# Order of the small tiled matmuls in a state-space block with adaptive layer norm: reversed groups, inter-chunk products behind C-B products, a ring of ten C buffers

## The chip, the cores and the metric

The kernel runs on one core of a Trainium2 chip. The metric is the device time of one launch in microseconds (us). Three runs of the kernel before took 587.96, 587.55 and 584.75 us; the median is 587.55 us.

## The reference

Four sequences (b) of 512 tokens with 256 channels go through one block. `mod` is computed from a condition vector; `xBC` goes through a causal convolution of four taps over the tokens; the scan has 32 heads of 8 channels with a state of 64; the feed-forward part has 1024 hidden channels and a Walsh-Hadamard transform.

```python
h = layernorm(x) * (1 + ca) + sa
xBC, z, A_log = split(h @ W_in.T)
x_, B, C = split(conv4(xBC) + conv_b)
a = -softplus(A_log)
L = exp(segsum(a))                              # lower triangle, 512 x 512 per head
M = einsum('blhn,bshn,bhls->bhls', C, B, L)
y = einsum('bhls,bshp->blhp', M, x_) + D * x_
x = x + ga * (y * silu(z + z_bias)) @ W_out.T
h = layernorm(x) * (1 + cb) + sb
x = x + gb * fwht(silu(h @ W1.T) * (h @ W3.T)) @ W2.T
```

All of it is in float32, and so is the output, (4, 512, 256).

## The kernel before

**Tiling.** The 512 x 512 matrices are never formed. Tokens are cut into 8 chunks of 64. Inside a chunk y comes from products of C and B with the decay (intra); between chunks a state of 64 x 8 per head is carried (states, a scan, inter). A projection (`proj`, L249) is six matmuls of 128 x 512 into one PSUM buffer: float32 is split in a high and a low part, and three of the four products are made for two halves of the 256 channels.

**Units, quads, pairs.** There are 8 units (i, b): half i of the heads, sequence b. A unit has two quads m; a quad has four pairs of heads. The pairs are numbered k from 0 to 63 over all units, four to a quad. So one step k is one pair, and one unit is eight steps.

**What a step does.** Names as they stand in the profile:

- `project(k, half)` (L432) makes B (tile pbc, L251) or C (tile pcc, L251) in PSUM. `conv` (L385) then convolves it into SBUF (bc or cc): ACT writes the first tap (L387) and a shifted copy cv (L389), DVE adds two taps (L390, L391) and with the second one has read the PSUM buffer for the last time, POOL adds cv (L392). Three PSUM buffers are shared by these projections and by px and pz. bc has a ring of 3 buffers and cc one of 8.
- `prep_l(k)` (L425): one matmul pl (L428) and ACT's Exp give the decay l (L430).
- `attend(k)`, at every odd k (L442): 64 small matmuls of 64 x 64 for the two pairs k-1 and k, in tiles pG (L262), each on a quarter of PE's array. They are chained in one order by `Chain` (L253). DVE then multiplies l by pG (L458).
- `turn_b(k)` (L460): four transposes bT (L464), copied by ACT to bt (L466).

**What a quad does,** after its four steps: `states(m)` (L525, tile ps, L530), 16 small matmuls on 32 columns each, needs bt of the four pairs and xwz; `intra(m)` (L537, tile py, L546), 32 small matmuls on 32 columns, needs l of the four pairs and xpad; `turn_states(m)` (L552) transposes the states (sT), DVE scans them over the chunks (sn, L559) and POOL masks them into sts (L563); `inter(m)` (L566, tile pi, L572), 28 small matmuls on 32 columns, needs sts and C of the quad's four pairs, whose buffers come free behind it.

**What a unit does.** `x_part2` and `x_part3` (L502 on) lay x out for the small products: transposes xt (L513), then DVE writes xpad (L517) and xwz (L520), for the two halves of the tokens one after the other. `gate_z` (L577) projects z (pz), and `gate_y` (L589) joins py, pi and the gate: DVE multiplies ex by pi (L593), where ex is the decay from the start of a chunk. For every sequence in the first four units a prologue does the layer norm (xn, L281), the transposes (pt, L291), and a softplus chain on ACT and DVE (pa, parts, L354). In the second four units `finish_unit` projects the output (po, L610) and prepares the second layer norm. Then come 32 steps of the feed-forward part (tile f, L251; tiles pdy and pdyi, L724), from about 456 us on.

**What sets the order.** Every step is put on an agenda with a due time in units of k (`T`, L399; the calls from L780), and the agenda is run in order of time. That gives the order in which instructions are issued. On PE, DVE, ACT and POOL a scheduler in the build then decides the final order from its own estimates of when operands are ready. It can't move an instruction ahead of one that it is told to stay behind: `behind(x)` (L85) puts what is issued inside it behind the recorded instruction `last[x]`. SP, which issues most DMAs, keeps the order of the agenda.

The lines around the change, as they stand before:

```python
        for n, pg in zip(ks, pgs):
            ve.tensor_tensor(lts[n], pg, lts[n], ALU.mult)
...
        for c in range(1, NC):
            for g in range(4):
                l = slice(Q * c, Q * c + Q)
                pe.matmul(pi[32 * g : 32 * g + 32, l], sts[pp][:, c - 1, g], ccs[4 * m + g][:, l],
```

Of the kernel before, what the change touches and what calls it, by code (L numbers as in the profile page):

```python
# [14 lines left out]
F32R = mybir.dt.float32r  # L15
BF16 = mybir.dt.bfloat16
AF = mybir.ActivationFunctionType
ALU = mybir.AluOpType
# [3 lines left out]
NB, S, DM = 4, 512, 256  # L22
NH, HD = 32, 8
Q = 64
NC = S // Q
# [5 lines left out]
def mamba_ffn(tc, ctx, u, c_t, wmod, win_t, cw, cb, zb, dsk, wo_t, w13_t, w2_t,  # L31
              k_ident, k_reset, k_dl, k_dr, k_had, k_own, out):
    nc = tc.nc
    ve, ac, gp, pe = nc.vector, nc.scalar, nc.gpsimd, nc.tensor
# [25 lines left out]
    def work(shape, name, tag, bufs=2, dtype=F32):  # L60
        return wk.tile(shape, dtype, name=name, tag=tag, bufs=bufs)

    def mtile(shape, name):
        return ps_m.tile(shape, F32, name=name, tag="m")

    def ptile(name):
        return ps_p.tile([128, S], F32, name=name, tag="p")
# [15 lines left out]
    last = {}  # L83

    def behind(*engines):  # L85
        stack = ExitStack()
        for e in engines:
            stack.enter_context(tc.issue_after(last[e].ins))
        return stack
# [67 lines left out]
    sts = [const.tile([128, NC - 1, 4, 32], F32, name=f"sts{pp}") for pp in range(2)]  # L157
# [36 lines left out]
    def fetch_quad(n, half, **kw):  # L194
        return fetch(win_t[:, 544 + 1024 * n : 544 + 1024 * n + 1024], 512 * half, 512, f"wq{n}", **kw)
# [53 lines left out]
    def proj(ps, w, c0, ht):  # L249
        for n, (a, b, k) in enumerate(TERMS):  # L250
            last[pe] = pe.matmul(ps, w[:, a, k, c0 : c0 + 128], ht[k][:, b], start=(n == 0), stop=(n == 5))  # L251
# [133 lines left out]
    def conv(ps, tl, dst):  # L385
        w = cw_sb[:, tl]
        ac.activation(dst, ps, AF.Identity, bias=cb_sb[:, tl : tl + 1], scale=w[:, 3:4])  # L387
        v = work([128, S], "cv", "cv", 3)
        last[ac] = ac.activation(v, ps, AF.Copy, scale=w[:, 0:1])  # L389
        ve.scalar_tensor_tensor(dst[:, 1:], ps[:, : S - 1], w[:, 2:3], dst[:, 1:], ALU.mult, ALU.add)  # L390
        last["conv"] = ve.scalar_tensor_tensor(dst[:, 2:], ps[:, : S - 2], w[:, 1:2], dst[:, 2:], ALU.mult, ALU.add)  # L391
        last[gp] = gp.tensor_tensor(dst[:, 3:], dst[:, 3:], v[:, : S - 3], ALU.add)  # L392
# [5 lines left out]

    T = dict(  # L399
        attend=0.12, turn_b=0.13, prep_l=-1.31, proj_b=-1.11, proj_c=-1, load_d=-3.13,  # L400
        states=-0.03, intra=0.1, turn=1.47, inter=2.53,
        x_proj=1.32, x0=-1.5, x1=2.12, x2=3.46, x3=3.77, gate_z=5.89, fin0=3.54, fin1=3.96, fin2=4.99, fin3=6.63,
        pro0=-11.83, pro1=-7.06, pro2=-4.93, pro3=-4.48, pro4=-3.88, next_ht=-3.77, pro04=0.27,
        quads=1.55, xz1=32.3, wo=19.68, mod=18.99, w2=40.89, wf0=56.74, wf1=62.02, wf2=62.29,
# [3 lines left out]
    def where(k):  # L408
        i, b = units[k // 8]
        return i, b, (k // 4) % 2, k % 4  # L410

    lts, bcs, ccs, bts, exs, des, xcs, xds, dcs, stt, pys, zts = ({} for _ in range(12))
# [19 lines left out]
    def project(k, half):  # L432
        i, b, pp, g = where(k)
        w = wq[2 * i + pp]
        tl = 2 + 8 * (2 * i + pp) + 2 * g
        dct, nm, nb = ((bcs, "bc", 3), (ccs, "cc", 8))[half]
        pb = ptile(f"p{nm}{k}")
        proj(pb, w, 256 * g + 128 * half, ht[i, b])
        dct[k] = work([128, S], f"{nm}{k}", nm, nb)
        conv(pb, tl + half, dct[k])  # L440

    def attend(k):  # L442


        ks = (k - 1, k)
        pgs = [mtile([128, S], f"pG{n}") for n in ks]
        chain = Chain()
        for c in range(NC):


            for n, pg in list(zip(ks, pgs))[::-1]:
                for j in range(2):
                    i, o = 64 * j, 64 * (j ^ (n % 2))
                    r, l = slice(i, i + 64), slice(Q * c, Q * c + Q)
                    chain.matmul(pg[o : o + 64, l], bcs[n][r, l], ccs[n][r, l], start=True, stop=True,
                                 tile_position=(i, o))
        for n, pg in zip(ks, pgs):
            ve.tensor_tensor(lts[n], pg, lts[n], ALU.mult)  # L458

    def turn_b(k):  # L460
        bc = bcs[k]
# [63 lines left out]
    def states(m):  # L525
        pp = m % 2
        pst = mtile([128, 4, 128], f"ps{m}")
        for t in range(4):
            for g in range(4):
                pe.matmul(pst[32 * g : 32 * g + 32, t], xwz[:, t, 4 * g + 2 * pp : 4 * g + 2 * pp + 2].rearrange("p h q x -> p (h q x)"),  # L530
                          bts[4 * m + g][:, t], start=True, stop=True, tile_position=(0, 32 * g))
        for g in range(4):
            bts.pop(4 * m + g)
        stt[m] = work([128, 4, 128], f"st{m}", "st", 1)
        ac.activation(stt[m], pst, AF.Copy)

    def intra(m):  # L537
        n, pp = divmod(m, 2)
        if pp == 0:
            pys[n] = (ps_1.tile([128, S], F32, name=f"py{n}", tag="y"),  # L540
                      ps_1.tile([128, S], F32, name=f"pi{n}", tag="yi"))
        py = pys[n][0]
        for c in range(NC):
            for g in range(4):
                l = slice(Q * c, Q * c + Q)
                pe.matmul(py[32 * g : 32 * g + 32, l], xpad[:, pp, c, g], lts[4 * m + g][:, l],  # L546
                          start=(pp == 0 and c == 0), stop=(pp == 1), skip_group_check=True,
                          tile_position=(0, 32 * g))
        for g in range(4):
            lts.pop(4 * m + g)  # L550
# [15 lines left out]
    def inter(m):  # L566
        n, pp = divmod(m, 2)
        pi = pys[n][1]
        for c in range(1, NC):
            for g in range(4):  # L570
                l = slice(Q * c, Q * c + Q)
                pe.matmul(pi[32 * g : 32 * g + 32, l], sts[pp][:, c - 1, g], ccs[4 * m + g][:, l],  # L572
                          start=(pp == 0 and c == 1), stop=(pp == 1), skip_group_check=True,
                          tile_position=(0, 32 * g))
        for g in range(4):
            ccs.pop(4 * m + g)

# [68 lines left out]
            split(wf[h], c0, 512, fetch(w13_t[:, 1024 * h : 1024 * h + 1024], c0, 512, f"wf{h}"))  # L646


    early = dict(tag="cc", bufs=8)
    q00 = fetch_quad(0, 0, **early)  # L650
    nc.sync.dma_start(wa, win_t[:, 512:544].rearrange("(k p) c -> p k c", p=128))
    cw_sb = cload(cw, [128, 34, 4], "cw_sb", nc.sync)
# [30 lines left out]
    for k in range(AHEAD):  # L683
        for half in range(2):
            with behind(pe, ve):
                project(k, half)
        if k == 1:
            with behind(ac):
                split_quad(1, 0, q10)
# [15 lines left out]
    def ffn_up(b, f):  # L705
        w = wf[f // 4]
        p1, p3 = ptile(f"f1{b}{f}"), ptile(f"f3{b}{f}")
        proj(p1, w, 256 * (f % 4), h2[b])
        proj(p3, w, 256 * (f % 4) + 128, h2[b])
        t = work([128, S], f"ft{b}{f}", "bt", 6)  # L710
        ac.activation(t, p1, AF.Tanh, scale=0.5)  # L711
        ve.scalar_tensor_tensor(t, t, 1.0, p1, ALU.add, ALU.mult)  # L712
        ve.tensor_tensor(t, t, p3, ALU.mult)  # L713
        hi = work([128, S], f"fh{b}{f}", "cc", 8, F32R)
        lo = work([128, S], f"fl{b}{f}", "cc", 8, F32R)
        ac.activation(hi, t, AF.Copy)  # L716
        (ve if (b, f) == (NB - 1, 7) else gp).tensor_tensor(lo, t, hi.bitcast(F32), ALU.subtract)  # L717
        return hi, lo
# [21 lines left out]
    def up(s_):  # L740
        hid[s_] = ffn_up(s_ // 8, s_ % 8)
# [38 lines left out]
    for m in range(16):  # L780
        at_time(4 * m + 4 + T["states"], states, m)
        at_time(4 * m + 4 + T["intra"], intra, m)
        at_time(4 * m + 4 + T["turn"], turn_states, m)
        at_time(4 * m + 4 + T["inter"], inter, m)
        if m:
            at_time(4 * m + T["load_d"], load_d, m)
    for k in range(NP):
        if k % 2:
            at_time(k + T["attend"], attend, k)
        at_time(k + T["turn_b"], turn_b, k)  # L790
        if k >= AHEAD:
            at_time(k + T["proj_b"], project, k, 0)
            at_time(k + T["proj_c"], project, k, 1)
        if k >= LOOK_P:
            at_time(k + T["prep_l"], prep_l, k)
# [112 lines left out]
```

## Time and profile before

| what | value |
|---|---|
| runs | 587.96, 587.55, 584.75 us |
| median | 587.55 us |
| profiled execution | 587.68 us |
| its span, first to last instruction | 585.9 us |
| mean granted clock of PE | 0.988 |
| PE, matmuls | 549.5 us busy |
| PE, weight loads (beside matmuls) | 432.6 us busy |
| DVE | 401.7 us busy |
| ACT | 387.2 us busy |
| POOL | 325.8 us busy |

Engines: PE multiplies matrices, DVE and ACT work elementwise (ACT with functions), POOL is a third elementwise engine, SP issues DMAs. L251 is line 251 of the kernel. A group line of a view has the line, the engine, and output and inputs by the program's names. In a row of the timeline the first number is the start in us from the start of the span and the second the length; "x6" are six instructions in a row, and a bracket at the end gives the idle time ahead of it and what ended it. In a row of the waits there are the engine and tile that waited, an arrow to what they waited for, the sum in us, how many times, and the longest one. In a row of the windows there are the stretch, its length, the busy time of PE, PE's weight loads, DVE, ACT and POOL (with instructions in brackets), the granted clock of PE, and the share and rate of the DMAs.

Some durations that come up: a tap on DVE takes 0.74 us (L390, L391), a product of l 0.68 us (L458), the scan of the states 1.21 us (L559), the four operations of xn on ACT 2.08 us (L281), the convolution's first tap on ACT 0.78 us (L387).

### The profile page before, as it was taken

What the parts mean: (1) busy time and instruction counts of PE and PEld (TensorE: products, weight loads), DVE (VectorE), ACT (ScalarE), POOL (GpSimd) and SP (SyncE); (2) the same over time, 40 slices, a digit from 0 to 9 for tenths busy, and PEclk for the clock granted to TensorE, in tenths of its full rate; (3) what the DMA queues carried; (4) which work ended last, traced back from release to release, by engine and by line L of the source; (5) the groups of instructions that cost most, each with busy time, mean ns of one, the idle gap of its engine ahead of it and who ended that gap; (6) DMA issues with size and microseconds to landing.
All of it is one profiled execution on the core that took longest, in us unless ns stands there. A gap on an engine that the chain in (4) does not pass through costs nothing.

```text
span 585.9 us, 16301 instructions
## 1 busy us (share of the span) xinstructions
PE 549.5 (94%) x6867; PEld 432.6 (74%) x6868; DVE 401.7 (69%) x672; ACT 387.2 (66%) x666; POOL 325.8 (56%) x299
## 2 busy tenths in 40 slices
PE   9868899899899989999999899899989999999996
PEld 5545686667687766877777677677767898888886
DVE  5978667977878675889787779787855454333243
ACT  5988779788966877896794787769584242232321
POOL 5862447435635668466465557477666645334341
PEclk9998999999999989999999899999989999999999
DMA  7351101401232343014103142164157037004021
GB/s 230 106 184 35 49 2 74 66 16 59 67 63 56 117 143 121 2 62 137 42 4 113 75 112 104 61 170 149 38 156 286 2 127 217 35 1 152 1 82 36
DMA packets 41793, 51.99 MB, mean 89 GB/s; under 512 B 17943, under 2 KB 29941, under 8 KB 41721
## 3 DMA queue, kind: packets, MB, share of 16 engines
q1 hardware_dynamic: 41448, 50.96, 28.5%
q8 instruction: 54, 0.88, 0.6%
q14 instruction: 19, 0.15, 0.1%
q10 hardware_dynamic: 272, 0.00, 0.0%
HBM read 33.51 MB, written 17.44 MB: 87 GB/s over the span
## 4 chain that ended last, share of the span: by engine, by line
PE 40%; DVE 5%; ACT 4%; POOL 2%; issue 1%; DMA 1%; POOLq 0%; DVEq 0%
PE f L251 15%; PE pcc L251 4%; PE pdy L724 4%; PE pdyi L724 4%; PE pbc L251 3%; PE po L610 2%; PE pG L262 1%; PE py L546 1%; PE bT L464 1%; ACT xn L281 1%; PE ps L530 1%; PE pi L572 1%; DVE cc L390 1%; DVE bc L390 1%; PE pt L291 1%
## 5 line engine op out<-in xcount | busy, mean ns | idle before, releaser
L392 POOL TENSOR_TENSOR bc<-bc,cv 128x509 f32<-128x509 f32 x64 | 69.6, 1088 | 55.8 <-DVE bc L391 37.9
L251 PE MATMUL f<-h,wf 128*128 128x512 f32 x384 | 97.7, 395 | 0.0
L392 POOL TENSOR_TENSOR cc<-cc,cv 128x509 f32<-128x509 f32 x64 | 69.7, 1090 | 50.1 <-DVE cc L391 39.1
L251 PEld LDWEIGHTS f<-h,wf 128*128 128x128 f32 x384 | 69.2, 190 | 12.5
L717 POOL TENSOR_TENSOR fl<-ft,fh 128x512 fp32r<-128x512 f32 x31 | 40.0, 1293 | 57.8 <-ACT fh L716 55.1
L390 DVE SCALAR_TENSOR_TENSOR cc<-pcc,cw_sb,cc 128x511 f32<-128x511 f32 x64 | 47.6, 743 | 32.2 <-ACT cv L389 32.1
L387 ACT ACTIVATE cc<-pcc,cb_sb,cw_sb 128x512 f32<-128x512 f32 x64 | 50.2, 784 | 22.8 <-PE pcc L251 17.3
L251 PE MATMUL pcc<-ht,wq 128*128 128x512 f32 x192 | 55.8, 424 | 6.1 <-DVE bc L391 6.1
L387 ACT ACTIVATE bc<-pbc,cb_sb,cw_sb 128x512 f32<-128x512 f32 x64 | 50.1, 782 | 15.4 <-PE pG L262 14.0
L716 ACT ACTIVATE fh<-ft 128x512 fp32r<-128x512 f32 x32 | 20.2, 631 | 57.6 <-DVE ft L713 27.7
L712 DVE SCALAR_TENSOR_TENSOR ft<-ft,f 128x512 f32<-128x512 f32 x32 | 21.9, 688 | 52.4 <-ACT ft L711 52.3
L251 PE MATMUL pcc<-hr,wq 128*128 128x512 f32 x192 | 54.5, 417 | 2.9 <-DVE bc L391 2.2
L390 DVE SCALAR_TENSOR_TENSOR bc<-pbc,cw_sb,bc 128x511 f32<-128x511 f32 x64 | 47.6, 744 | 11.1 <-ACT cv L389 10.8
L251 PE MATMUL pbc<-hr,wq 128*128 128x512 f32 x192 | 52.4, 406 | 1.4 <-DVE cc L391 1.0
L251 PE MATMUL pbc<-ht,wq 128*128 128x512 f32 x192 | 51.7, 402 | 1.6 <-DVE bc L391 1.6
L251 PEld LDWEIGHTS pcc<-ht,wq 128*128 128x128 f32 x192 | 35.7, 196 | 19.1 <-DVE bc L391 7.0
L391 DVE SCALAR_TENSOR_TENSOR bc<-pbc,cw_sb,bc 128x510 f32<-128x510 f32 x64 | 47.5, 743 | 1.2
L391 DVE SCALAR_TENSOR_TENSOR cc<-pcc,cw_sb,cc 128x510 f32<-128x510 f32 x64 | 47.6, 743 | 1.0
L458 DVE TENSOR_TENSOR l<-pG,l 128x512 f32<-128x512 f32 x64 | 41.2, 683 | 8.3 <-PE pG L262 7.9
L464 PE MATMUL bT<-ident,bc 128*128 128x128 f32 x256 | 41.2, 283 | 4.6 <-ACT bt L466 2.4
L466 ACT ACTIVATE bt<-bT 128x512 f32<-128x512 f32 x64 | 38.8, 606 | 9.8 <-PE bT L464 9.5
L262 PEld LDWEIGHTS pG<-cc,bc 64*64 64x64 f32 x2048 | 34.8, 134 | 13.7 <-issue 9.7
(154 smaller groups left out, 1244.8 us busy)
## 6 DMA issues: line engine op xcount, KB each, us to landing
wq<-win_t SPq DMA_DIRECT2D x16, 256.0 KB
htd<-ht SPq DMA_DIRECT2D x8, 512.0 KB
hr<-htd SPq DMA_DIRECT2D x8, 512.0 KB
h2d<-ht SPq DMA_DIRECT2D x8, 512.0 KB
h<-h2d SPq DMA_DIRECT2D x8, 512.0 KB
x<-u SPq DMA_DIRECT2D x7, 512.0 KB
ex<-pd SPq DMA_DIRECT2D x8, 256.0 KB
ygd<-yg SPq DMA_DIRECT2D x4, 512.0 KB
```

The lines of the kernel that those rows point to most:

```text
L251: last[pe] = pe.matmul(ps, w[:, a, k, c0 : c0 + 128], ht[k][:, b], start=(n == 0), stop=(n == 5))
L262: self.before = pe.matmul(*args, **kw)
L387: ac.activation(dst, ps, AF.Identity, bias=cb_sb[:, tl : tl + 1], scale=w[:, 3:4])
L390: ve.scalar_tensor_tensor(dst[:, 1:], ps[:, : S - 1], w[:, 2:3], dst[:, 1:], ALU.mult, ALU.add)
L391: last["conv"] = ve.scalar_tensor_tensor(dst[:, 2:], ps[:, : S - 2], w[:, 1:2], dst[:, 2:], ALU.mult, ALU.add)
L392: last[gp] = gp.tensor_tensor(dst[:, 3:], dst[:, 3:], v[:, : S - 3], ALU.add)
L458: ve.tensor_tensor(lts[n], pg, lts[n], ALU.mult)
L464: pe.transpose(pt[:, t], bc[:, 128 * t : 128 * t + 128], ident)
L466: ac.activation(bts[k], pt, AF.Copy)
L712: ve.scalar_tensor_tensor(t, t, 1.0, p1, ALU.add, ALU.mult)
L717: (ve if (b, f) == (NB - 1, 7) else gp).tensor_tensor(lo, t, hi.bitcast(F32), ALU.subtract)
L724: last[pe] = pe.matmul(pds[t // 2][:, t % 2], hid[a][:, tok], w2h[f][:, w_], start=(f == 0 and t % 2 == 0 and m == 0), stop=(f == 7 and m ...
```

## The change

- The due time of `inter` goes from 2.53 to 3.13 steps after the quad, and its matmuls are put behind the last matmul of the latest `attend`, which `attend` now records.
- The ring of C goes from 8 buffers to 10. Early weight loads and the feed-forward part's hidden tiles, which use the same ring, are named with 10 too.
- `attend` multiplies l of the second pair first, and l of the first pair is put behind that.
- `states` goes through t and g backwards; `intra` goes through the chunks backwards and through the pairs in the order 2, 3, 0, 1, so that the matmul that starts the accumulation (`start`) is that of the last chunk.

In the changed file the lines behind L457 stand 2 to 5 lines further down.

```diff
--- before.py
+++ after.py
@@ -398,7 +398,7 @@
 
     T = dict(
         attend=0.12, turn_b=0.13, prep_l=-1.31, proj_b=-1.11, proj_c=-1, load_d=-3.13,
-        states=-0.03, intra=0.1, turn=1.47, inter=2.53,
+        states=-0.03, intra=0.1, turn=1.47, inter=3.13,
         x_proj=1.32, x0=-1.5, x1=2.12, x2=3.46, x3=3.77, gate_z=5.89, fin0=3.54, fin1=3.96, fin2=4.99, fin3=6.63,
         pro0=-11.83, pro1=-7.06, pro2=-4.93, pro3=-4.48, pro4=-3.88, next_ht=-3.77, pro04=0.27,
         quads=1.55, xz1=32.3, wo=19.68, mod=18.99, w2=40.89, wf0=56.74, wf1=62.02, wf2=62.29,
@@ -433,7 +433,7 @@
         i, b, pp, g = where(k)
         w = wq[2 * i + pp]
         tl = 2 + 8 * (2 * i + pp) + 2 * g
-        dct, nm, nb = ((bcs, "bc", 3), (ccs, "cc", 8))[half]
+        dct, nm, nb = ((bcs, "bc", 3), (ccs, "cc", 10))[half]
         pb = ptile(f"p{nm}{k}")
         proj(pb, w, 256 * g + 128 * half, ht[i, b])
         dct[k] = work([128, S], f"{nm}{k}", nm, nb)
@@ -454,8 +454,10 @@
                     r, l = slice(i, i + 64), slice(Q * c, Q * c + Q)
                     chain.matmul(pg[o : o + 64, l], bcs[n][r, l], ccs[n][r, l], start=True, stop=True,
                                  tile_position=(i, o))
-        for n, pg in zip(ks, pgs):
-            ve.tensor_tensor(lts[n], pg, lts[n], ALU.mult)
+        last["pG"] = chain.before
+        last["l"] = ve.tensor_tensor(lts[k], pgs[1], lts[k], ALU.mult)
+        with behind("l"):
+            ve.tensor_tensor(lts[k - 1], pgs[0], lts[k - 1], ALU.mult)
 
     def turn_b(k):
         bc = bcs[k]
@@ -525,8 +527,9 @@
     def states(m):
         pp = m % 2
         pst = mtile([128, 4, 128], f"ps{m}")
-        for t in range(4):
-            for g in range(4):
+
+        for t in range(4)[::-1]:
+            for g in range(4)[::-1]:
                 pe.matmul(pst[32 * g : 32 * g + 32, t], xwz[:, t, 4 * g + 2 * pp : 4 * g + 2 * pp + 2].rearrange("p h q x -> p (h q x)"),
                           bts[4 * m + g][:, t], start=True, stop=True, tile_position=(0, 32 * g))
         for g in range(4):
@@ -540,11 +543,11 @@
             pys[n] = (ps_1.tile([128, S], F32, name=f"py{n}", tag="y"),
                       ps_1.tile([128, S], F32, name=f"pi{n}", tag="yi"))
         py = pys[n][0]
-        for c in range(NC):
-            for g in range(4):
+        for c in range(NC)[::-1]:
+            for g in (2, 3, 0, 1):
                 l = slice(Q * c, Q * c + Q)
                 pe.matmul(py[32 * g : 32 * g + 32, l], xpad[:, pp, c, g], lts[4 * m + g][:, l],
-                          start=(pp == 0 and c == 0), stop=(pp == 1), skip_group_check=True,
+                          start=(pp == 0 and c == NC - 1), stop=(pp == 1), skip_group_check=True,
                           tile_position=(0, 32 * g))
         for g in range(4):
             lts.pop(4 * m + g)
@@ -566,12 +569,14 @@
     def inter(m):
         n, pp = divmod(m, 2)
         pi = pys[n][1]
-        for c in range(1, NC):
-            for g in range(4):
-                l = slice(Q * c, Q * c + Q)
-                pe.matmul(pi[32 * g : 32 * g + 32, l], sts[pp][:, c - 1, g], ccs[4 * m + g][:, l],
-                          start=(pp == 0 and c == 1), stop=(pp == 1), skip_group_check=True,
-                          tile_position=(0, 32 * g))
+
+        with behind("pG"):
+            for c in range(1, NC):
+                for g in range(4):
+                    l = slice(Q * c, Q * c + Q)
+                    pe.matmul(pi[32 * g : 32 * g + 32, l], sts[pp][:, c - 1, g], ccs[4 * m + g][:, l],
+                              start=(pp == 0 and c == 1), stop=(pp == 1), skip_group_check=True,
+                              tile_position=(0, 32 * g))
         for g in range(4):
             ccs.pop(4 * m + g)
 
@@ -646,7 +651,7 @@
             split(wf[h], c0, 512, fetch(w13_t[:, 1024 * h : 1024 * h + 1024], c0, 512, f"wf{h}"))
 
 
-    early = dict(tag="cc", bufs=8)
+    early = dict(tag="cc", bufs=10)
     q00 = fetch_quad(0, 0, **early)
     nc.sync.dma_start(wa, win_t[:, 512:544].rearrange("(k p) c -> p k c", p=128))
     cw_sb = cload(cw, [128, 34, 4], "cw_sb", nc.sync)
@@ -711,8 +716,8 @@
         ac.activation(t, p1, AF.Tanh, scale=0.5)
         ve.scalar_tensor_tensor(t, t, 1.0, p1, ALU.add, ALU.mult)
         ve.tensor_tensor(t, t, p3, ALU.mult)
-        hi = work([128, S], f"fh{b}{f}", "cc", 8, F32R)
-        lo = work([128, S], f"fl{b}{f}", "cc", 8, F32R)
+        hi = work([128, S], f"fh{b}{f}", "cc", 10, F32R)
+        lo = work([128, S], f"fl{b}{f}", "cc", 10, F32R)
         ac.activation(hi, t, AF.Copy)
         (ve if (b, f) == (NB - 1, 7) else gp).tensor_tensor(lo, t, hi.bitcast(F32), ALU.subtract)
         return hi, lo
```

## Prediction

> **What bounds it now.** The head of the page and its first part come first: the busy time of each engine over the span.
>
> ```profile
> span 585.9 us, 16301 instructions
> PE 549.5 (94%) x6867; PEld 432.6 (74%) x6868; DVE 401.7 (69%) x672; ACT 387.2 (66%) x666; POOL 325.8 (56%) x299
> ```
>
> PE works 94% of the span, so the kernel is bound by PE's own time, and a change can gain in two ways: by making the busy stretch shorter, or by taking from the 36 us in which PE stands idle. The profiled execution took 587.68 us, 1.8 us of it outside the span; that is 0.1 us above the median of the three runs (587.55), so I count from 587.68 and correct nothing.
>
> The granted clock by stretches comes next, because idle PE can be paid for twice.
>
> ```profile
> 49.40:52.80 3.40, 1.53 (x9) 0.90 (x9) 3.17 (x7) 3.17 (x6) 0.00 (x0) 1.00 0.19 43
> 52.90:56.30 3.40, 3.40 (x10) 2.58 (x10) 3.40 (x8) 3.39 (x7) 1.94 (x2) 0.50 0.21 27
> 72.00:456.00 384.00, 365.31 (x5575) 281.21 (x5574) 296.77 (x480) 292.14 (x503) 232.09 (x213) 0.99 0.29 88
> ```
>
> The column of 0.50 and 1.00 is PE's clock. After a stretch with 1.53 us of work in 3.40 came one at half clock. The same 0.50 stands for 3.4 us at 209.9, 325.95 and 435.2 us, each time behind a PE wait of 1.4 to 1.7 us. Such a window costs up to 1.7 us (half of 3.4). From 72 to 456 us PE is busy 365.3 of 384 us and no other engine is over 297.
>
> The Trainium skill ("TensorE: Matmul & The Clock Gate", Part 1) gives a free-running window of 3413 ns and an idle window as the condition for half clock; the rows agree on the length, but here a window that was 45% busy was enough.
>
> **What a change of matmul shape costs.** PE's timeline gives the price. Columns: start, length, then the line and tile. I read start to start, since ends are modelled.
>
> ```profile
> 14.23 1.52 PE L251 MATMUL pbc<-ht,wq 128*128 128x512 f32 x6
> 15.59 1.52 PE L251 MATMUL pcc<-ht,wq 128*128 128x512 f32 x6
> 16.95 1.52 PE L251 MATMUL px<-ht,wxz 128*128 128x512 f32 x6
> ```
>
> Six full matmuls with full ones before and behind: 1.36 us.
>
> ```profile
> 176.79 0.39 PE L428 MATMUL pl<-dr,dl 94*128 94x512 bf16 x1
> 177.12 0.99 PE L572 MATMUL pi<-cc,sts 128*32 128x64 f32 x56
> 178.04 1.65 PE L251 MATMUL pbc<-ht,wq 128*128 128x512 f32 x6
> 179.53 1.52 PE L251 MATMUL pcc<-ht,wq 128*128 128x512 f32 x6
> 180.98 1.16 PE L262 MATMUL pG<-cc,bc 64*64 64x64 f32 x64
> 182.07 0.66 PE L464 MATMUL bT<-ident,bc 128*128 128x128 f32 x4
> ```
>
> The same six take 1.49 us behind pi (178.04 to 179.53), whose matmuls use 32 columns of the array, and 1.45 when pG follows, whose matmuls use a quarter of it (179.53 to 180.98). So entering the small shapes costs 0.09 us, and the first full matmul after them about 0.11 more than a clean one. The single records give the rest: the last small matmul to the next full one is 149 ns against 16 ns between small ones, so leaving costs 0.133; the first transpose behind small ones costs 0.055 more.
>
> **The order.** From the order of instructions in both built programs I counted the runs of equal shape on PE. Entries into small shapes from full ones fall from 94 to 67, because pi (L572), which stood alone between full products, goes behind pG, and because py (L546) and ps (L530) no longer stand in fragments around pw, pbc and bT (py's runs 53 to 32, ps's 31 to 18). Changes out of a small shape fall from 97 to 82; the 82 include 15 places pG to pi. First full matmuls behind a small one fall from 33 to 23, first transposes from 56 to 44.
>
> - entering: 27 x 0.09 = 2.43 us
> - leaving: 15 x 0.133 = 2.00 us
> - first full: 10 x 0.106 = 1.06 us
> - first transpose: 12 x 0.055 = 0.66 us
>
> Together **6.15 us** less PE time. Bounds: 4.4 if only entering and leaving are real and the first matmuls' lateness is part of them (2.43 + 2.00); 8.1 if pG to pi is free (15 x 0.133 = 2.0 more). Pi to pG is seen three times, at 150 ns against 15; pG to pi is not seen. I charge it the full 0.133, by that nearest row.
>
> The Trainium skill ("TensorEngine Tiling (Array Packing)", Key Properties) says that "Changing tiling mode (not just tile) drains the TensorE", which speaks against part of the change: pG (64 x 64) and pi (128 x 32) are two modes. By the rule the sum is 6.15, without it 8.1; the pi-to-pG row is on its side.
>
> **Ten buffers for C.** The waits view shows ACT waiting for pi at the start of the convolution of C: the ninth C needs the buffer that pi of the old quad still reads.
>
> ```profile
> PE pcc L251 <- DVE bc L391: 8.4, 14, 2.4
> ACT cc L387 <- PE pi L572: 4.8, 7, 1.9
> PE pt L291 <- ACT bt L466: 3.4, 2, 1.7
> PE xt L513 <- DVE l L458: 1.5, 1, 1.5
> ```
>
> Two more buffers let pi stand later by about half a step (2.53 to 3.13). Without them the 4.8 us on ACT would grow by about a pbc and a pcc of PE time (2.8 us) each of 15 times. With them it goes. ACT is busy 292 of 384 us, so the 4.8 us is not on PE's path: 0.
>
> **Edits that I cost at nothing.** States and intra issue the same matmuls backwards; py's start flag moves to the last chunk with the order. Instructions on PE that carry a wait fall from 611 to 579, and no row shows a price for a wait already met: 0. The two products on DVE (2 x 0.68 us, L458) change places: 0 by themselves. Moved steps issue no DMAs, so SP's queue is as before; POOL's product that makes the states (L563, 1.02 us) gets 1.3 us more time before pi reads them. The FFN's order, from about 456 us, is nearly the same: 0.
>
> **What is late next.** Intra now starts with the last chunk and pair, so PE can't fill a wait with half of py. In the first half of a unit py needs xpad of both halves of x. Unit 1 shows where that matters:
>
> ```profile
> 105.69 0.75 DVE L391 SCALAR_TENSOR_TENSOR bc<-pbc,cw_sb,bc 128x510 f32<-128x510 f32 x1
> 106.50 1.66 PE L251 MATMUL pcc<-ht,wq 128*128 128x512 f32 x6 [0.48 <-DVE bc L391]
> ```
>
> This pcc (pair 14) takes the PSUM buffer that the second tap of B of pair 13 frees. In the changed order DVE has the softplus chain, both l products (fixed in order, one behind the other) and the product with ex, which needs pi, ahead of that tap. Going through the new order by hand with the old durations, I get 108.6 instead of 106.5: **+2.1 us**, seen from the old time. The following waits (py for both xpads, 114.5; pz 117.1 instead of 113.84; pair 16's pcc 127.75 instead of 123.62) would make it +4.1 by the unit's end; unit 2 gives +3.0 by the same path. Those pass through three engines' orders, where one operation placed otherwise undoes them. So the two units cost between 0 and 7.1 us beyond the savings; the row nearest to them, PE's wait for B's tap, has a mean of 0.6 us (8.4 over 14) and a longest of 2.4. I take 2.1, the one wait that the order names directly, which is inside that row.
>
> Sum: 587.68 - 6.15 + 2.1 = 583.63, so **583.6 us**, 0.7% faster. A measurement of this kernel can tell about 0.5% (2.9 us) from no change.
>
> **Rivals.**
>
> 1. **More is gained.** pG to pi is free (8.1), unit 1's wait finds cover, and one of the four half-clock windows goes (up to 1.7): 587.68 - 8.1 - 1.7 = 577.9. For it: the wait of 1.49 us ahead of the window at 209.9 is for l, which the change moves. Against it: two other windows stand behind ACT's bt, which is not touched.
> 2. **The saving is given back; no change.** The shapes switch less, but PE waits for the same producer a little longer: a switch saved ahead of a DVE wait is no time. Units 1 and 2 cost 7.1 in full: 587.68 - 6.15 + 7.1 = 588.6. This is also how it would look if the change doesn't do what it says and the switches mostly lay beside waits. For it: DVE and ACT are the releasers of most PE waits. Against it: between 72 and 456 us PE has only 13.5 us of such idle time in the timeline's gaps.
> 3. **Slower, by the fixed order on DVE.** The l products chained to each other and ex behind pi hold B's taps, at the first half of units 1 and 2; the idle time is 7.1 us, and since single gaps pass 1.4 us there, two further half-clock windows follow (2 x 1.7), with entering and leaving alone saved (4.4): 587.68 - 4.4 + 7.1 + 3.4 = 593.8. It decides as soon as added idle time and half-clock loss exceed 6.15 + 2.9 = 9.1 us (7.3 with the small saving). For it: at 1.4 to 1.7 us all four such gaps led into 0.50. Against it: from unit 3 on, by the same hand trace, every first half gains 0.4 to 1.2 us.
>
> **Numbers.** My forecast, faster by 0.5 to about 1.2%: 0.42. More gained: 0.08. No change: 0.24. Slower by over 0.5%: 0.26. Faster together 0.50. The forecast's own range is 580.5 to 584.7; since cases of both signs hold much of the chance, the range for 8 in 10 goes from rival 1 (578) to just short of rival 3's full price, 593.
>
> **What would show it.** Right: PE's busy time falls by 4 to 8 us with the same number of matmuls; the timeline has pG followed by pi in one stretch, py and ps in runs; ACT no longer waits for pi; PE's wait for B's tap grows by 2 to 3 us in unit 1 only. Rival 2: PE's busy time falls and its idle time rises by as much. Rival 3: new 0.50 stretches between 105 and 165 us, and pairs 14, 16 and 22 wait over 1.4 us for DVE. Wrong altogether: PE's busy time doesn't fall, so a switch isn't a price of its own; or pG to pi costs over 0.3 us.

## The result, and the profile after

The changed kernel took 603.15 us in the median of five runs (599.91 to 604.45), the kernel before 584.75 us (584.04 to 587.96) beside it: a ratio of 1.0288, with a 95% interval of 1.0243 to 1.0332. The forecast was 583.6 us, the range 578 to 593. It is slower, and by more than the rival that said so.

The head of the page of the changed kernel:

```profile
span 601.4 us, 16275 instructions
PE 550.5 (92%) x6868; PEld 439.6 (73%) x6868; DVE 399.8 (66%) x672; ACT 388.4 (65%) x666; POOL 325.0 (54%) x299
```

PE's busy time is 1.0 us longer, although it was to fall. That line hides two opposite changes, so I took PE's trace apart, from its first matmul to the end of its last. *Idle* is the sum of the gaps between matmuls. *Clock* is half of the time that PE was busy inside stretches with a granted clock of 0.50. *Work* is the rest: what the matmuls would take at full clock.

| profiled execution | time | work | idle | clock | mean granted clock |
|---|---|---|---|---|---|
| before | 587.68 | 542.9 | 30.3 | 6.6 | 0.988 |
| changed | 603.15 | 534.6 | 44.8 | 15.9 | 0.971 |
| difference | +15.5 | -8.3 | +14.5 | +9.3 | |

The three differences add up to the whole between the two profiles. The medians are 18.4 us apart: the profile of the kernel before is that of a run 2.9 us above its median, and these 2.9 us are not split here. The clock term isn't an accident of one profile: over the five runs the mean clock is 0.971, over 77 runs of the kernel before 0.988 (a 78th, of 2922.72 us, is left out), and (1 - 0.971) x 602.6 - (1 - 0.988) x 585.9 is some 10 to 11 us.

**The saving is there.** PE's timeline in unit 3 shows the order that the change asks for: pbc and pcc in one stretch, then pG, then pi.

```profile
190.69 1.52 PE L251 MATMUL pcc<-ht,wq 128*128 128x512 f32 x6
192.14 1.16 PE L262 MATMUL pG<-cc,bc 64*64 64x64 f32 x64
193.23 0.99 PE L577 MATMUL pi<-cc,sts 128*32 128x64 f32 x56
194.15 0.66 PE L466 MATMUL bT<-ident,bc 128*128 128x128 f32 x4
```

From the last pG to the first pi it is 148 ns (median of 15), as much as from pi to pG before.

**The clock.** These are rows of the windows view of the changed kernel. The second column is the length, the third PE's busy time; then come the other engines, the granted clock, and the DMAs.

```profile
108.60:112.00 3.40, 1.05 (x6) 0.47 (x5) 3.40 (x9) 3.37 (x5) 2.18 (x2) 1.00 0.00 0
112.02:115.43 3.41, 3.41 (x8) 2.73 (x9) 3.41 (x10) 1.42 (x4) 3.41 (x4) 0.50 0.23 57
...
234.90:238.30 3.40, 0.63 (x4) 0.49 (x5) 2.19 (x3) 3.40 (x7) 1.47 (x3) 1.00 0.32 93
238.32:241.73 3.41, 2.98 (x7) 1.91 (x7) 3.03 (x5) 3.08 (x7) 3.41 (x4) 0.50 0.47 127
241.74:245.14 3.40, 3.40 (x10) 2.63 (x9) 0.90 (x2) 1.87 (x3) 3.40 (x4) 0.50 0.77 266
```

Two stretches in which PE worked 1.05 and 0.63 us of 3.4 are each followed by half clock; after the second, one window wasn't enough. Up to its last matmul the changed kernel has ten such windows, the kernel before four.

**Where PE waits.** PE's idle time by stretch, bounded by the pl of the given pairs:

| stretch | before | changed |
|---|---|---|
| pairs 2 to 8 (unit 0) | 8.74 | 10.30 |
| 12 to 16 (first half of unit 1) | 2.89 | 5.76 |
| 20 to 24 (first half of unit 2) | 1.35 | 3.66 |
| 24 to 28 | 0.00 | 1.52 |
| 28 to 32 | 2.94 | 4.69 |
| 32 to 63 | 7.71 | 9.52 |
| 63 to the end | 1.98 | 5.72 |

In the stretches left out (up to pair 2, 8 to 12, 16 to 20) PE idles 1.0 us less than before in all. The waits view names the producers (us in total, times, longest):

```profile
PE pcc L251 <- DVE bc L391: 9.7, 8, 2.4
PE bT L466 <- ACT bt L468: 7.8, 6, 3.1
...
PE po L615 <- DMA yr<-ygd: 2.8, 1, 2.8
```

Of the second line the kernel before has this, and of the third none:

```profile
PE bT L464 <- ACT bt L466: 2.4, 4, 0.8
```

ACT's wait for pi is gone, as forecast. The timeline of the first half of unit 1 shows the first line at work:

```profile
107.66 0.68 DVE L458 TENSOR_TENSOR l<-pG,l 128x512 f32<-128x512 f32 x1
...
108.25 0.68 DVE L460 TENSOR_TENSOR l<-pG,l 128x512 f32<-128x512 f32 x1
...
109.05 0.61 DVE L598 TENSOR_TENSOR ex<-ex,pi 128x448 f32<-128x448 f32 x1
...
109.58 0.74 DVE L390 SCALAR_TENSOR_TENSOR bc<-pbc,cw_sb,bc 128x511 f32<-128x511 f32 x1
...
110.44 0.74 DVE L390 SCALAR_TENSOR_TENSOR cc<-pcc,cw_sb,cc 128x511 f32<-128x511 f32 x1
...
111.09 0.74 DVE L391 SCALAR_TENSOR_TENSOR bc<-pbc,cw_sb,bc 128x510 f32<-128x510 f32 x1
...
111.98 2.86 PE L251 MATMUL pcc<-ht,wq 128*128 128x512 f32 x6 [1.61 <-DVE bc L391]
```

Both l products, ex and a tap of C stand ahead of the second tap of B, and pair 14's pcc waits 1.61 us for it. It then takes 2.86 us instead of 1.66, because the half-clock window begins at 112.0.

The second wait line comes over a queue that the prediction had set aside. SP's queue and what hangs on it, ahead of 237 us:

```profile
225.54 0.34 SPq L848 DMA_DIRECT2D ygd<-yg  x1
...
225.94 2.03 SPq L175 DMA_DIRECT2D wq<-win_t  x2
...
229.30 0.90 SPq L175 DMA_DIRECT2D wxz<-win_t  x2
...
233.91 0.92 ACT L184 ACTIVATE wxz<-wxz 128x256 fp32r<-128x256 f32 x2 [1.01 <-DMA wxz<-win_t]
...
237.29 0.63 PE L466 MATMUL bT<-ident,bc 128*128 128x128 f32 x4 [3.14 <-ACT bt L468]
```

The store of the gated output (ygd) needs ex, which needs pi. It stands ahead of the loads of the next weights. In the kernel before it was issued 10.9 us behind pair 28's pl (199.58):

```profile
210.44 0.34 SPq L843 DMA_DIRECT2D ygd<-yg  x1
```

Now it is issued 13.8 us behind it (211.72). So the weights are asked for later, ACT waits for them (1.01 us), and PE waits for ACT. How much of the 3.14 us comes from the store is a question for spill_later, below.

### The profile page after: what moved, and what is told of

Same layout as the page of the kernel before. It is cut to its first block, busy times and chain, and to the rows that moved or that the text cites. A ratio compares the mean times of both kernels' runs of the same rounds, so it can differ in the third digit from the quotient of the medians.

```text
span 601.4 us, 16275 instructions
## 1 busy us (share of the span) xinstructions
PE 550.5 (92%) x6868; PEld 439.6 (73%) x6868; DVE 399.8 (66%) x672; ACT 388.4 (65%) x666; POOL 325.0 (54%) x299
## 4 chain that ended last, share of the span: by engine, by line
PE 56%; DVE 16%; ACT 15%; DMA 4%; issue 3%; POOL 3%; SPq 1%; POOLq 0%; DVEq 0%; ACTq 0%
PE f L251 13%; PE pcc L251 9%; PE pbc L251 8%; PE pdyi L729 4%; PE pdy L729 4%; PE pG L262 3%; ACT cv L389 3%; PE bT L466 2%; DVE bc L390 2%; DVE cc L390 2%; DVE bc L391 2%; ACT bc L387 2%; PE py L549 2%; PE ps L533 2%; DVE sn L562 2%
## 5 line engine op out<-in xcount | busy, mean ns | idle before, releaser
L251 PE MATMUL pcc<-ht,wq 128*128 128x512 f32 x192 | 57.3, 437 | 9.3 <-DVE bc L391 8.7
L387 ACT ACTIVATE bc<-pbc,cb_sb,cw_sb 128x512 f32<-128x512 f32 x64 | 50.3, 787 | 13.5 <-PE pG L262 11.4
L251 PE MATMUL pbc<-ht,wq 128*128 128x512 f32 x192 | 55.6, 426 | 2.8 <-ACT l L430 2.3
L251 PEld LDWEIGHTS pcc<-ht,wq 128*128 128x128 f32 x192 | 37.9, 205 | 22.9 <-DVE bc L391 5.3
L251 PEld LDWEIGHTS pbc<-ht,wq 128*128 128x128 f32 x192 | 38.0, 203 | 12.9 <-ACT l L430 2.7
L466 PEld LDWEIGHTS bT<-ident,bc 128*128 128x128 f32 x256 | 28.2, 142 | 22.7 <-issue 11.6
```

The costliest lines, as they stand in the source:

```text
L466: pe.transpose(pt[:, t], bc[:, 128 * t : 128 * t + 128], ident)
```

## The experiments

All ratios are to the kernel before, run beside each. Work, idle and clock are those of one profile each, whose run can lie up to 3.7 us off the median.

| run | median us | ratio, 95% interval | work | idle | clock |
|---|---|---|---|---|---|
| only_loops | 592.73 | 1.0127 (1.0087 to 1.0167) | 535.4 | 39.5 | 9.9 |
| only_states_loop | 591.50 | 1.0092 (1.0057 to 1.0126) | 539.6 | 33.8 | 10.2 |
| only_intra_loop | 588.07 | 1.0027 (0.9996 to 1.0058) | 539.6 | 33.8 | 3.4 |
| second_quads_only | 585.83 | 1.0014 (0.9985 to 1.0043) | 540.4 | 30.7 | 5.0 |
| only_inter | 598.63 | 1.0219 (1.0179 to 1.0259) | 540.0 | 39.9 | 11.3 |
| only_l_order | 585.32 | 1.0023 (0.9987 to 1.0058) | 542.4 | 30.0 | 5.1 |
| only_ten_buffers | 589.30 | 1.0042 (1.0003 to 1.0081) | 543.2 | 32.5 | 6.8 |
| undo_loops | 598.63 | 1.0209 (1.0156 to 1.0262) | 541.3 | 39.3 | 11.4 |
| undo_inter | 592.61 | 1.0109 (1.0051 to 1.0168) | 535.6 | 40.4 | 6.1 |
| undo_l_order | 604.87 | 1.0337 (1.0270 to 1.0404) | 534.0 | 45.4 | 17.3 |
| undo_ten_buffers | 618.16 | 1.0531 (1.0488 to 1.0575) | 536.2 | 56.4 | 15.6 |
| softplus_first | 601.28 | 1.0282 (1.0201 to 1.0363) | 534.5 | 43.6 | 13.4 |
| softplus_first_ex_late | 603.88 | 1.0321 (1.0251 to 1.0392) | 533.3 | 43.5 | 17.0 |
| taps_first | 604.70 | 1.0317 (1.0265 to 1.0369) | 535.3 | 44.3 | 17.9 |
| spill_later | 600.01 | 1.0251 (1.0182 to 1.0321) | 533.2 | 43.0 | 14.5 |
| named_causes_undone | 597.54 | 1.0207 (1.0161 to 1.0254) | 536.4 | 38.8 | 13.2 |
| fill_before | 587.79 | 1.0050 (1.0024 to 1.0075) | 549.6 | 28.9 | 5.1 |
| fill_changed | 600.63 | 1.0247 (1.0196 to 1.0298) | 548.1 | 39.3 | 4.3 |

### One part alone

only_loops has the hunks of `states` and `intra` alone; only_inter those of `inter` and the ten buffers; only_l_order and only_ten_buffers one hunk each.

> The kernel before with one edit: states and intra go through their loops backwards. Theory W (waits by fixed orders): the longer time of the changed kernel is PE idle time (44.8 us against 30.3 between matmuls) plus the half-clock windows that follow it (34.1 us against 13.7), made by pi behind pG, with ex behind pi on DVE, and by the chained l products; the saving in changes of shape is real. Then the loops alone only save: entries into small shapes 94 to 73, 21 x (0.09 + 0.133) + 6 x 0.106 + 10 x 0.055 = 5.9 us less, about 579 to 581 us. Rival L (loops): starting with the operand that is ready last takes from PE the work that it used to do during waits; the loops alone then bring most of the added idle time, 590 to 600 us.

> The kernel before with two edits: pi due at 3.13 and held behind pG, and ten buffers of C (pi can't be moved so far with eight). Entries 94 to 84, but 15 changes pG to pi, so about 1 us less PE time. W: the ex product on DVE, which needs pi, holds the second tap of B in the first halves of units 1 and 2: 588 to 594 us. L: no loss, 583 to 585 us.

> The kernel before with one edit: DVE multiplies l of the second pair first and l of the first pair behind it. PE's order is as before. W: up to 3 us slower if the chain holds other work of DVE, 585 to 588 us. L: 584 to 586 us.

> The kernel before with one edit: ten buffers for C instead of eight. PE's order is as before but for one entry. Both theories: 584 to 586 us, and ACT no longer waits for pi (4.8 us before).

Theory W (fixed orders, with pi behind pG) and theory L (the loops) both hold, each for a part. The order of l does nothing that can be told. Pi behind pG with ten buffers costs 12 us: W expected 588 to 594, and it is more, since idle rises by 9.6 and clock by 4.6 while work falls by 2.9. The loops alone cost 7 us although their work falls by 7.5: idle rises by 9.2. So W's forecast for the loops (579 to 581) was wrong. Ten buffers alone cost 0 to 0.8%.

What the loops do shows in the timeline of only_loops in unit 1:

```profile
113.20 0.67 DVE L517 TENSOR_TENSOR xpad<-xt,own 128x512 f32<-128x512 f32 x1
...
113.93 1.02 PE L547 MATMUL py<-l,xpad 128*32 128x64 f32 x57 [2.84 <-DVE xpad L517]
```

Py begins with the last chunk, so it waits 2.84 us for xpad of the second half of x. In the kernel before 28 matmuls of py and half of ps were done between 108.5 and 109.7 us, ahead of the second xpad (111.0 us):

```profile
108.52 0.64 PE L546 MATMUL py<-l,xpad 128*32 128x64 f32 x28
```

### One part undone

> The changed kernel with the loops of states and intra forwards again. Theory W (waits by fixed orders, pi behind pG and the chained l products): the waits stay and the saving in shapes gets smaller (entries 67 to 84, 17 x 0.223 + 3 x 0.106 + 12 x 0.055 = 4.8 us more): 603 to 609 us. Rival L (loops): most of the added idle time goes, 585 to 592 us.

> The changed kernel with pi due at 2.53 again and not held behind pG; loops, order of l and ten buffers stay. W: the waits go and the saving in shapes stays (entries 73 against 94 before): 580 to 586 us. L: 598 to 604 us.

> The changed kernel with the two l products in the first order and not chained. PE's counts are those of the changed kernel. W: if the chain is part of the cause, 597 to 601 us; if not, 602 to 604. L: 602 to 604 us.

> The changed kernel with eight buffers for C. Both theories: ACT's first convolution step of the ninth C waits for pi, which now stands later, and PE waits for it in turn: 605 to 620 us.

The answers agree with the parts: without the loops' edit 598.63 (only_inter: 598.63), without inter's 592.61 (only_loops: 592.73), and l's order makes no difference. W and L had each put nearly the whole loss on one part, so each missed one of the first two. Together the two losses, 12 and 7 us, are about the whole 18. PE's idle time does not add up in this way: it rises by 9.6 and 9.2 us alone and by 14.5 together. In the first halves of units 1 and 2 either part alone brings it from 4.2 us to 9.0 (only_inter) or 10.5 (only_loops), and both together to 9.4. The waits there stand in for each other: pcc of pairs 14 and 22 waits 1.6 us in only_inter, py 2.84 and 2.38 us in only_loops. So with one part undone there is about as much idle time left there (10.0 us in undo_inter, 10.1 in undo_loops). Ten buffers are needed for pi's new place: with eight it is 618.16 us, and PE's idle time 56.4.

### Which loop, and where

only_states_loop and only_intra_loop have one hunk each. In second_quads_only pp is the quad in its unit, and the start flag is as before:

```diff
-        for t in range(4):
-            for g in range(4):
+        for t in range(4)[::1 - 2 * pp]:
+            for g in range(4)[::1 - 2 * pp]:
...
-        for c in range(NC):
-            for g in range(4):
+        for c in range(NC)[::1 - 2 * pp]:
+            for g in ((0, 1, 2, 3), (2, 3, 0, 1))[pp]:
```

> The kernel before with one edit: intra goes through the chunks backwards and the pairs in the order 2, 3, 0, 1; states as before. Theory L (py can't start on the first half of x): PE waits for xpad ahead of py in units 1 and 2, 2 to 3 us each as in only_loops, and the time is that of only_loops or a little more, 590 to 595 us. Rival: the reversed states loop makes the waits; then 581 to 585 us (entries 94 to 79).

> The kernel before with one edit: states goes through t and g backwards; intra as before. Entries 94 to 89. If the loss of only_loops needs both loops (py can still fill the wait for the second half of x): 584 to 587 us and no PE wait over 1 us ahead of py in units 1 and 2. If the states loop alone makes it: 589 to 593 us.

> The kernel before, with the loops of states and intra backwards in the second quad of a unit only. Entries 94 to 86, first transposes 56 to 49: 8 x 0.223 + 7 x 0.055 = 2.2 us less work. If the waits of only_loops come from the first quads alone, PE's idle time stays at 30 to 31 us: 581 to 584 us. If moving shapes costs waits there too: 585 to 590 us.

One loop alone leaves PE the other to work on while it waits: idle rises by 3.5 us with either, by 9.2 with both. The intra loop's 588.07 us lies between its two expectations, and its ratio can't be told from 1. The states loop's 591.5 us is above what I expected for the joint case, so it also costs by itself: 0.86 us of wait ahead of py in unit 1, and two half-clock windows more. The 3.4 us of clock in the profile of only_intra_loop is low for this kernel: its mean clock over ten runs is 0.985, against 0.989 for the kernel before beside it. With the loops backwards in the second quads alone, idle is 30.7 against 30.3 us: the waits come from the first quads, where the second half of x is late. So the idle time is what the first theory said, but the time (585.83 us) lies in the rival's range: the 2.5 us of saved work that it keeps don't show in the median, which is the same within half a per cent.

### What holds the tap, and the store

softplus_first, softplus_first_ex_late and taps_first undo single orders in units 1 and 2:

```diff
-            last[ac] = ac.activation(e, e, AF.Ln, bias=1.0)
+            last[ac] = last["soft"] = ac.activation(e, e, AF.Ln, bias=1.0)
...
-        conv(pb, tl + half, dct[k])
+        if k in (13, 21) and half:
+            with behind("soft"):
+                conv(pb, tl + half, dct[k])
+        else:
+            conv(pb, tl + half, dct[k])
```

The second adds `behind("conv")` to ex in units 0 and 1, due 0.7 steps later. taps_first instead adds `behind("conv")` to the first tap of C of those pairs. spill_later issues the store later:

```diff
-                after(2, nc.sync.dma_start, ygd[b], ygt.pop((0, b)).bitcast(F32))
+                after(5, nc.sync.dma_start, ygd[b], ygt.pop((0, b)).bitcast(F32))
```

> The changed kernel with one instruction on ACT held back: in units 1 and 2 the first convolution step of C of the sixth pair (13 and 21) stands behind the last step of the softplus chain again, as before the change. The orders of PE and DVE are those of the changed kernel. Theory W1: ACT's order holds the chain on DVE, which stands ahead of the second tap of B; then PE's waits for that tap at pairs 14 and 22 (1.61 us each) fall by about 0.8 us, and the half-clock windows behind them (3.4 and 6.8 us) go or get shorter: 597 to 601 us. Rival W2: the l products and ex on DVE hold the tap, and ACT doesn't matter: 602 to 604 us.

> As softplus_first, and in units 0 and 1 the product of ex with pi on DVE is due 0.7 steps later and held behind the latest convolution, so that it leaves the path to B's tap. Both W1 and W2: the waits at pairs 14 and 22 are near the 0.48 us of the kernel before, no half-clock window follows: 594 to 600 us. If waits or windows stay, the cause is elsewhere.

> As softplus_first, and in units 1 and 2 DVE's first tap of C (pairs 13 and 21) stands behind the second tap of B. Theory T: in the changed order the tap of B that PE waits for stands behind a tap of C, which itself waits for ACT; then the wait at pairs 14 and 22 (1.61 us) falls to 0.9 us or less: 597 to 601 us. Rival: l and ex alone hold it; then it stays at 1.6 us.

> The changed kernel with one edit: the store of a finished unit's gated output (ygd) is issued on SP three steps later in the order, so that it doesn't stand ahead of the weight loads of the next half. Theory S: pi being later makes the gated output later, its store waits at the head of SP's queue, the weights behind it come later, ACT waits for them and PE for ACT: the wait of 3.14 us ahead of bT at 237 us falls to about 1 us and the half-clock windows at 238 us (6.8 us) go: 597 to 600 us. Rival: the loads wait for their own buffers, no change: 602 to 604 us.

With softplus_first the wait ahead of pl 13 (0.97 us) falls to 0.40, but pair 14 still waits 1.61, and that is the wait that W1 had named: W1 failed on it. With ex late it waits 2.08 us, so that expectation failed too. With the taps in order the wait is 0.35 us, and the tap no longer ends it, as theory T said; but py, 8 us later, now waits 1.90 us for xpad, and the time is not in T's range. The idle time of unit 1's first half goes 5.76, 5.20, 4.58, 4.14 through these three; that of unit 2's stays between 3.3 and 4.2. No median can be told from the changed kernel's. The wait is passed on: DVE is busy through that stretch (3.40 of 3.40 us in the window at 108.6), which speaks for each order only choosing what PE waits for.

Theory S is not shown. The wait that it named does fall, as the timeline of spill_later has it:

```profile
234.69 0.63 PE L466 MATMUL bT<-ident,bc 128*128 128x128 f32 x4 [1.58 <-ACT bt L468]
```

The wait of 3.14 us is 1.58, one half-clock window follows instead of two, and PE's wait for yr at the tail falls from 2.81 to 1.56. But the same wait is shorter in other runs too, with the store in its old place: 1.82 us in taps_first (236.47 us), 1.83 in softplus_first_ex_late (234.60) and 1.59 in only_inter (233.12). In the kernel before it was 0.22 (225.42). So the place of the store is one link in the queue, and its share of the wait stays open. The median is 3 us lower, less than the intervals can tell.

### The clock by itself, and the causes together

The fill runs repeat a matmul that writes the same result again, by `for _ in range(1 + n)` around pl or bT. named_causes_undone joins the loops of second_quads_only, taps_first and spill_later, and keeps the rest of the change.

> The changed kernel with the same kind of fill ahead of its long waits: pl of pairs 4, 5, 7, 13, 15, 21, 24, 31, 47, 55 and 63 four to ten times more, the transposes of pair 57 twice more. Theory C: the half-clock windows fall from ten to four or fewer, the idle time between matmuls falls since the fill takes its place: 592 to 598 us. Rival: the time is lost to waiting anyway, and the windows cost nothing beyond it: 602 to 606 us.

> The kernel before, with PE kept busy in its long waits by matmuls that write the same result again: pl of pairs 4, 5 and 29 six, five and six times more (0.2 us each), the transposes bT of pairs 46 and 62 three times more. Theory C (clock): a window of 3.4 us with less than about half of it busy is followed by one at half clock, and the extra work only uses time in which PE stood idle; then two or more of the four half-clock windows go, each worth 1.7 us: 579 to 583 us. Rival: the windows come anyway, or the extra work costs its time (up to 5 us): 585 to 591 us.

> The changed kernel, with pi behind pG and ten buffers kept, and with the named causes undone: the loops backwards only in the second quad of a unit, where xpad has long been ready, forwards in the first; the softplus step and the taps as in taps_first; the store of the gated output later, as in spill_later. Entries 75 against 94 before and 67 in the changed kernel. If the causes are these, PE's idle time falls from 44.8 to 36 us or less, with 2 to 5 half-clock windows: 584 to 592 us. If something else carries the loss, idle time stays above 40 us: 596 us or more.

In fill_changed the extra matmuls cost 13.5 us of work and took the place of only 5.5 us of idle, yet the kernel is not slower than the changed one: the clock term fell from 15.9 to 4.3, with three windows for ten. The mean clock of its four runs is 0.989. The time, 600.63, is above the 592 to 598 expected, since I had taken the fill as free. So half clock is a cost of its own: 11.6 us less of it paid for the rest of the fill. Of the loss it is 9.3 us by the two profiles, 10 to 11 by the runs' mean clocks. In fill_before the fill costs more than the clock gives back (work +6.7, idle -1.4, clock -1.5, in a run 3.7 us above the median): theory C's range was missed, with three windows left of four.

named_causes_undone takes back 5.6 of the 18 us, not the 11 or more expected. Idle falls to 38.8 us. What stays sits behind pair 28 (4.59 against 2.94 before) and after pair 63 (5.74 against 1.98): a PE wait of 2.23 us for ACT's bc at 216.6, of 2.67 for bt, and of 2.9 for yr. None of the three was undone by itself, so their cause stays open. Pi's new place alone is not it: after pair 63 only_inter has 4.70 us of idle and only_loops 3.02, but second_quads_only, which leaves pi where it was, has 4.26, with a wait of 1.47 us for yr.

No version here beats the kernel before. A rival is untested: except for inter's, every due time of the agenda stayed at the value that it had in the kernel before. The runs moved only those of gate_y in units 0 and 1 (softplus_first_ex_late) and of the store. How much of the loss would go with due times made for the new order is not shown.

## Why the prediction was wrong

- **The saving in shapes** was forecast at 6.15 us, between 4.4 and 8.1. Measured: 8.3 us less work. Right in kind, and a little more. Pi behind pG does pay its 148 ns, so the 2 us beyond the sum are not the free change that I had kept as the upper bound; what they are stays open.
- **The sum "587.68 - 6.15 + 2.1" puts all waiting at 2.1 us. This is the step that failed.** In its place the two profiles show 14.5 us more idle time and 9.3 us more half clock. The next three points are its parts.
- **"So the two units cost between 0 and 7.1 us beyond the savings [...] I take 2.1".** The first halves of units 1 and 2 added 5.2 us of idle time (2.87 and 2.31), nearer to the hand trace's full price than to the 2.1. The orders of the hand trace were those of the profile: pair 14 waits for B's tap behind l, l and ex. But the prediction kept one of its waits and dropped the rest, because one operation placed otherwise would undo them. That wait grew from 0.48 to 1.61 us, and pair 22's likewise, where 2 to 3 us in unit 1 alone were forecast.
- **The rest of the kernel** was put at nothing, or forecast to gain ("from unit 3 on [...] every first half gains"). PE idled longer by 1.56 us in unit 0, 1.52 in pairs 24 to 28, 1.75 in 28 to 32, 1.8 in 32 to 63 and 3.7 behind them. In each of the five first halves from unit 3 on it idled 0.2 to 1.5 us longer.
- **Half clock** was at nothing in the sum; it stood in the slower rival with two further windows, 3.4 us. It was six more, 9.3 us: idle time rose by half, the windows from four to ten. The reading "at 1.4 to 1.7 us all four such gaps led into 0.50" also left out a fifth: a wait of 1.58 us (up to 31.6 us) led into none, nor did the longer ones of 2.52 and 2.37 us (up to 23.2 and 40.8 us).
- **"Moved steps issue no DMAs, so SP's queue is as before"** was wrong. Inter issues none, but gate_y needs pi and ends in one, ahead of the weights in SP's queue; its issue came 2.9 us later behind pair 28's pl. What that cost is not shown: the wait at 237 us is 1.56 us shorter with the store moved, but also 1.3 us shorter in two runs without that.
- **What is late next**: "PE can't fill a wait with half of py" was the right mechanism, and it was priced only through unit 1's later waits. By the runs the loops bring 9.2 us of idle time alone (39.5 against 30.3) and 5.5 on top of the rest (44.8 against 39.3 in undo_loops).
- **Order of l, FFN at nothing**: the l order was right. For the FFN, from about 456 us, I had written "nearly the same: 0". Behind pair 63 PE idled 3.7 us longer: pt waits 1.0 us longer for ACT's bt, and po 2.8 us for yr.
- **Ten buffers at nothing** were right for ACT's wait, and needed, but alone they took 0 to 0.8%.

Rival 3 had the sign and a part of the mechanism (fixed orders, B's taps, half clock); the loops and the rest of the kernel were not in it, and its price of 593.8 was 9 us short.

## What to carry to other kernels

When a step moves, follow its consumers to the end of their chain: what they feed may stand in an in-order queue ahead of something else, as the store did ahead of the weight loads. Beginning with the operand that is ready last costs no waits only where that operand is early anyway (the second quads here); elsewhere the half that is ready is what the engine has to work on. Waits of two causes at one place can stand in for each other, so undoing one of them says little of its price. On PE price a wait twice, as itself and as the half-clock window that it may bring.

## What the runs showed of the hardware

- **Half clock comes on a fixed grid.** In the kernel before its windows begin at 52.88, 209.89, 325.95 and 435.17 us: 46, 34 and 32 times 3.413 us apart. Of the grid's full-clock windows in both profiles, all that were followed by half clock had PE busy for 1.85 us or less (the four in the kernel before: 1.56, 1.70, 1.75 and 1.85); none at 1.86 or more was, though four at 1.53 to 1.84 us escaped. So some 1.6 us of idle time can be enough if it falls inside one window. The same gap of 2.37 us near 40 us brought half clock in the profile after and not in that of before, where the grid cut it otherwise. This is no sharp rule: in the other 18 profiles half clock also followed windows with 1.88, 1.90 (undo_loops) and 2.12 us busy (only_states_loop), three windows near the start with 2.94 to 3.05, and one without any gap (only_intra_loop, 169.4 us); and one with 1.44 us escaped (only_inter).
- **A half-clock window lasts on** when PE is not busy in it: in these two profiles those with 2.68 to 2.98 us busy were followed by a second one, those with 3.05 or more by full clock. In the others the two overlap: 3.02 us was followed by a second (only_inter), 2.74 by full clock (undo_inter).
- **This is most of the scatter.** Over the 77 runs of the kernel before, time (582.96 to 591.0 us) and mean clock (0.997 to 0.977) have a correlation of -0.86.
- **Busy time can't be compared across clocks**: PE's went up by 1.0 us while its work went down by 8.3.
